# A graph layer on one Trainium2 core: a new order for the first blocks of edges

## Chip, core and metric

One core of a Trainium2 chip runs the whole kernel in one launch. The time is the device time of an execution in microseconds (us). The kernel before was run three times: 2399.72, 2402.55 and 2406.02 us, median 2402.55. The execution that was profiled took 2402.95 us, with a span of 2401.2 us from the first to the last instruction. Five engines work side by side, each in the order of its own instructions: TensorE (PE), VectorE (DVE), ScalarE (ACT), GpSimd (POOL) and SyncE (SP, which only issues transfers here).

## The reference

One layer of message passing over 12500 nodes with 64 features and 212500 edges, sorted by dst:

```python
h = jnp.maximum(_layernorm(x, axis=-1), 0.0)
edge_in = jnp.concatenate([h[src], h[dst], dist], axis=1)
e = silu(edge_in @ eW1 + eb1)
e = silu(e @ eW2 + eb2)
agg = segment_sum(e, src, num_segments=N)
out = silu(concatenate([h, agg], axis=1) @ nW1 + nb1) @ nW2 + nb2
return x + out
```

The first product is split: `eW1` has a part A for the source, a part B for the destination and a row for `dist`. A and B are multiplied with the nodes' h once, and each edge adds a row of A[src], a row of B[dst], dist times the last row, and eb1.

## The kernel before, in words

**Two halves.** Edges come sorted by destination but must be summed by source. So the kernel first *sends*: for each block of 1024 edges it gathers B's rows of their destinations, adds the share of dist and the bias, and scatters the 1024 rows into a table `q` in DRAM that is ordered by the bucket of the source (100 buckets of 125 nodes). Then *steps* load tiles of `q`, add A's rows, apply the two layers of SiLU and sum by node (`s_pt`, `s_p2`, `s_seg`, `s_add`). The buckets' places in `q` fill up level by level (14 levels), so steps of an early level run while later blocks are still being sent.

**A block.** 208 blocks of 1024 edges, two to a *pair*. `load(s)` fetches for a pair, by a base row number that SP reads from `base_i` (L355), the window `win` of B's rows: 2 x 60 rows at 4 offsets each, out of `tb0` for the first 30 blocks and out of `tb` later (L360). `load_rows(s)` puts two rows of edge weights (`ewH`, the weight rounded for the matmul, and `ewR`, what the rounding left) into `extras`, out of a DRAM copy `ews` (L335). `count(s)` finds each edge's row in q on VectorE: one-hot of the bucket (`oh`), its sum (`each`), a running count on TensorE (`upto`), the rank and the row number `to`; and it makes `pick`, the one-hot of the destination in the window plus the weight rows (L376). `send(s)` multiplies pick with win on TensorE (`qp`, L454), copies it to one of eight buffers `qs` on ScalarE (L466, L469), and issues one indirect write for each 128 edges on POOL (L476): 8 in a block, 1661 in all.

**The tables.** x is loaded in chunks of 12 nodes per partition (`xs`, three buffers), normed on VectorE and ScalarE (`norm`), turned on TensorE (`turned`, L682), and multiplied by A and B (`product`, L220 to L227); `ta`, `tb` and the h for the last layer `hd` are written to DRAM. Since the first blocks can't wait for all of it, the first 16 x 128 = 2048 nodes have a start of their own: `x0`, `first_rows(g)` for g = 0, 4, 8, 12, and a table `tb0` of B's rows alone (L696).

**The order** is written out by hand. PE, DVE, ACT and SP run their instructions in the order in which the program writes them (`manual_schedule`); only POOL's is chosen by the scheduler. Generators yield between stretches of work. The list `order` (L829 to L831) mixes the norm and the first rows, the sources' buckets (`sources(0)`, L768 to L781), the destinations (`destinations`, L744 to L763, which also makes `lo`, `base_i` and `rowsD`), the edge weights (`edge_weights`, L786 to L789: ewH on ScalarE, ewR - ewH and the two writes of ews on POOL) and then the first 1024 columns of the second half of the sources. Then come the small weights (POOL), the window of block 0, its count, and `send_all(0, 8)`: blocks 0 to 7, three pieces to a block, after each piece four steps of `feed`, which is the tables' work three chunks wide (`turns`), with `checks` after 48 steps. After these 24 pieces the bias of the second layer, `b2f`, is loaded and spread over 128 partitions by two matmuls of a row of ones and two copies (L854 to L859). A second stage of 39 pieces (blocks 8 to 20) follows with three feed steps to a piece, and then the main loop, in which pieces and steps alternate by a fixed plan of goals per level.

`checks` looks on VectorE whether every window held its destinations (two reductions over 104 x 2048, L796); if not, a general way at the end takes over, which these inputs don't need.

The eight `qs` are used in turn, so ScalarE's copy of a block's half waits until the indirect writes of eight halves ago have landed. Three buffers with the tag `rows` serve all of `got` and `rows_a`.

Of the kernel before, what the change touches and what calls it, by code (L numbers as in the profile page):

```python
# [34 lines left out]
OP = mybir.AluOpType  # L35
# [42 lines left out]
def tile_gnn(ctx: ExitStack, tc: tile.TileContext, x, src, dst, ew, eW1, eb1, eW2, eb2, nW1, nb1, nW2, nb2, out):  # L78
# [47 lines left out]
    CH = 12  # L126
    NE, EARLY = 16, 30
    x_rows = x.rearrange("(l b) d -> l b d", b=NB)
# [18 lines left out]
    nc.scalar.activation(warm, ones[:, 0:1], AF.Sqrt)  # L147
    nc.sync.dma_start(x0, x[: NE * P, :].rearrange("(p j) d -> p j d", j=NE))
    vec = lambda v, lo_, n, m: bass.AP(tensor=v.tensor, offset=v.offset + lo_, ap=[[m, n], [1, m]])
# [58 lines left out]

    tb0 = dram.tile([P * NE, 2 * H], F32, name="tb0")
    ta_buckets, tb_buckets = (t.rearrange("(l b) f -> l b f", b=NB) for t in (ta, tb))  # L210

# [39 lines left out]
    nb2b = const.tile([P, D], F32, name="nb2b")  # L251

    def later_weights():

        nc.gpsimd.dma_start(w2, eW2)
        nc.gpsimd.dma_start(w1g, nW1[D:, :])
        nc.gpsimd.dma_start(w2n, nW2)
        nc.gpsimd.dma_start(nb1c, bass.AP(tensor=nb1.tensor, offset=nb1.offset, ap=[[1, P], [1, 1]]))
        nc.gpsimd.dma_start(nb2b, rows_of(nb2, P))
        for a in range(2):  # L260
            nc.gpsimd.dma_start(w1n[a * D : (a + 1) * D, :], nW1[:D, :])
# [42 lines left out]
    with ExitStack() as work:  # L304
# [23 lines left out]
        def load_rows(s):  # L328

            if s < nblocks:  # L330
                p, g = s // 2, s % 2
                if g == 0:
                    for a in range(2):
                        at = a * HB + WL
                        nc.sync.dma_start(extras[p % 2][at : at + 2], ews[:, p, :, a])  # L335
# [11 lines left out]
        def load(s):  # L347

            if s < nblocks:
                p, g = s // 2, s % 2  # L350
                win = wins[p % NW]
                table, end = (tb0, NE * P) if s < EARLY else (tb, NB * P)
                assert s < EARLY or len(done_b) == NB // G
                if g == 0:
# [334 lines left out]
        def first_rows(g):  # L689

            hr = turned(x0, g)
            yield
            got = fp.tile([P, G, 2, H], F32, name="got", tag="rows")
            yield from product(1, hr, mm, "mm", got)
            yield
            nc.sync.dma_start(  # L696
                tb0.rearrange("(p j) f -> p j f", j=NE)[:, g : g + G, :], got.rearrange("p g k h -> p g (k h)")
            )
            yield
# [42 lines left out]
        def destinations():  # L742

            lim = lp.tile([NP, 1], F32, name="lim")  # L744
            nc.vector.tensor_scalar(lim, part[:NP], EARLY / 2 - 0.5, float((NB - NE) * P), op0=OP.is_gt, op1=OP.mult)
            nc.vector.tensor_scalar(lim, lim, float(NE * P - SPAN), None, op0=OP.add)
            nc.scalar.copy(f, dstR)
# [44 lines left out]
        def checks():  # L792

            ends = lp.tile([NP, 2, 4], F32, name="ends")
            for i, (op, sign, limit) in enumerate(((OP.max, 1.0, WL - 0.5), (OP.min, -1.0, 0.5))):
                nc.vector.tensor_reduce(ends[:, i, :], fv, AX.X, op)  # L796
                nc.vector.tensor_tensor(ends[:, i, :], ends[:, i, :], lo, op=OP.subtract)
# [20 lines left out]
        with listing:  # L818
            todo = groups()
            for _ in range(2):  # L820
                list(todo.pop(0))
            lists_, rows_, src0, src1, weights = destinations(), norm(x0, NE), sources(0), sources(1), edge_weights()
            made = [first_rows(g) for g in range(0, NE, G)]
            next(rows_)
# [26 lines left out]
        aggT = aggp.tile([P, NB, L], F32, name="aggT")  # L851
        b2f = aggp.tile([P, G, H], F32, name="b2f")
        eb2r = b2f[0:1, 0, :]
        for t in range(G):  # L854
            nc.sync.dma_start(b2f[0:1, t, :], rows_of(eb2, 1))
        for _ in range(2):
            p2 = p2p.tile([P, G, H], F32, name="p2")
            nc.tensor.matmul(p2, ones, b2f[0:1], start=True, stop=True)
            nc.scalar.copy(b2f, p2)  # L859
        ld2 = work.enter_context(tc.tile_pool(name="ld2", bufs=NQ))  # L860
# [197 lines left out]
```

## Time and profile before

| what | value |
|---|---|
| profiled execution / its span | 2402.95 us / 2401.2 us |
| median of three runs (lowest, highest) | 2402.55 us (2399.72, 2406.02) |
| busy: PE / DVE / ACT / POOL | 2084.7 / 1807.1 / 1316.8 / 1655.6 us |
| chain that ended last, by engine | PE 43%, DMA 19%, POOL 10%, DVE 7%, issue 5%, ACT 4% |
| DRAM traffic | 572.33 MB, mean 238 GB/s |
| first and last indirect write (L476) | start at 43.52 and 2209.16 us |

How to read it: a row of the timeline gives start, duration (both us), engine, line, operation, `out<-in`, and in brackets how long the engine had been idle and what ended that. A row of the waits gives the total us, the number of times and the longest. A row of the groups gives the line, engine, operation, names and count, then busy us, mean ns of one, and the idle time before it with its causes. A row of the windows gives the stretch and its length, then the engines' busy time in it with the number of instructions, the granted TensorE clock, the mean share of the DMA engines and GB/s. "SPq" is a transfer's issue on SP's queue. Buffer numbers are left out of names, so `tb` can be tb0, and `x` x0.

### The profile page before, as it was taken

How to read it: one execution, taken by the hardware profiler on the slowest of the kernel's cores; microseconds unless marked ns; L12 is line 12 of the kernel's file. 1: busy time of each engine (PE TensorE's matmuls, PEld its weight loads, DVE VectorE, ACT ScalarE, POOL GpSimd, SP SyncE). 2: the span in 40 equal slices, each digit the busy share in tenths (PEclk: the TensorE clock that was granted, in tenths of full speed). 3: DMA queues.
4: the chain of work that ended last, by engine and by line, in shares of the span. 5: the costliest groups of instructions: out<-in, count | busy, mean ns of one | idle time of the engine just before them, and what ended most of it. 6: DMA issues, size and time to landing. Idle time of an engine off the chain costs nothing.

```text
span 2401.2 us, 47870 instructions
## 1 busy us (share of the span) xinstructions
PE 2084.7 (87%) x17025; PEld 1909.0 (80%) x17025; DVE 1807.1 (75%) x2852; ACT 1316.8 (55%) x2861; POOL 1655.6 (69%) x1723
## 2 busy tenths in 40 slices
PE   3777887666688889988999999999999999999997
PEld 2555676655588788888888999998999999999885
DVE  7989977766678787776877667899988888875221
ACT  3333444333355566656666767666666666666543
POOL 5667777777777777777777766777777777776110
PEclk9555698877889999999999999999999999999999
DMA  5565877666677666777777777988888888888663
GB/s 161 210 235 212 274 227 236 209 209 220 210 250 253 209 225 221 225 236 255 258 259 247 264 251 254 294 262 255 269 269 275 266 267 279 263 270 269 207 187 92
DMA packets 238859, 572.33 MB, mean 238 GB/s; under 512 B 46346, under 2 KB 98534, under 8 KB 238097
## 3 DMA queue, kind: packets, MB, share of 16 engines
q1 hardware_dynamic: 154598, 390.24, 51.8%
q0 software_dynamic: 54080, 124.64, 14.2%
q10 hardware_dynamic: 29936, 54.31, 6.9%
q8 instruction: 138, 2.26, 0.4%
q14 instruction: 107, 0.88, 0.1%
HBM read 356.62 MB, written 212.35 MB: 237 GB/s over the span
## 4 chain that ended last, share of the span: by engine, by line
PE 43%; DMA 19%; POOL 10%; DVE 7%; issue 5%; ACT 4%; SPq 1%; ACTq 0%; POOLq 0%; DVEq 0%
DMA q<-qs,to 16%; PE seg L636 10%; POOL q L476 10%; PE p L622 10%; PE pt L583 9%; PE pt L576 5%; PE qp L454 4%; PE lr L562 3%; DMA out_dram<-os 2%; PE bc L344 1%; ACT qs L466 1%; DVE one L605 1%; SPq L124 1%; ACT e L592 1%; DVE rank L414 1%
## 5 line engine op out<-in xcount | busy, mean ns | idle before, releaser
L476 POOL DMA_INDIRECT q<-qs,to x1661 | 1615.7, 973 | 565.5 <-issue 398.4
L583 PE MATMUL pt<-oneT,a 125*128 125x128 f32 (+1 forms) x2800 | 433.9, 293 | 143.1 <-ACT oneT L567 142.1
L592 ACT ACTIVATE e<-pt 128x512 f32<-128x512 f32 x450 | 268.8, 597 | 477.4 <-PE pt L583 471.9
L622 PE MATMUL p<-w,e 128*128 128x128 f32 x3600 | 513.4, 287 | 0.0
L636 PE MATMUL seg<-one,e 128*128 128x125 f32 x3600 | 508.9, 285 | 0.2 <-DVE aggT L647 0.2
L583 PEld LDWEIGHTS pt<-oneT,a 125*128 125x128 f32 x2800 | 365.8, 198 | 159.5 <-ACT oneT L567 157.8
L622 PEld LDWEIGHTS p<-w,e 128*128 128x128 f32 x3600 | 457.6, 198 | 22.4 <-issue 22.4
L636 PEld LDWEIGHTS seg<-one,e 128*128 128x128 f32 x3600 | 445.3, 195 | 28.7 <-issue 27.3
L466 ACT COPY qs<-qp 128x512 f32<-128x512 f32 x418 | 244.5, 586 | 392.3 <-DMA q<-qs,to 276.1
L647 DVE TENSOR_TENSOR aggT<-aggT,seg 128x500 f32<-128x500 f32 x325 | 218.5, 672 | 210.1 <-PE seg L636 208.0
L454 PE MATMUL qp<-win,pick 128*128 128x256 f32 x1664 | 329.1, 325 | 28.3 <-DVE pick L376 10.8
L605 DVE TENSOR_TENSOR one<-misc,qt 128x500 f32<-128x500 f32 x450 | 302.7, 673 | 60.0 <-PE seg L636 33.1
L395 DVE TENSOR_REDUCE each<-oh 128x100 bf16<-128x800 bf16 x208 | 321.1, 1544 | 7.2
L454 PEld LDWEIGHTS qp<-win,pick 128*128 128x128 f32 x1664 | 254.1, 213 | 48.2 <-issue 15.1
L576 PE MATMUL pt<-ident,qt 128*128 128x128 f32 x1800 | 276.5, 277 | 8.3 <-ACT qs L466 7.9
L626 ACT ACTIVATE e<-p 128x512 f32<-128x512 f32 x450 | 268.7, 597 | 25.6 <-PE p L622 25.2
L567 ACT CAST oneT<-lr 125x512 fp32r<-125x512 f32 x450 | 264.7, 588 | 12.8 <-PE lr L562 12.4
L616 ACT COPY p<-b2f 128x512 f32<-128x512 f32 x450 | 267.2, 594 | 0.0
L576 PEld LDWEIGHTS pt<-ident,qt 128*128 128x128 f32 x1800 | 209.6, 143 | 23.7 <-issue 12.2
L414 DVE TENSOR_REDUCE rank<-terms 128x8 f32<-128x864 f32 x208 | 219.0, 1053 | 7.2
L376 DVE SCALAR_TENSOR_TENSOR pick<-bc,same,extra 128x512 fp32r<-128x512 f32 x208 | 154.6, 743 | 82.4 <-PE bc L344 54.3
L412 DVE TENSOR_TENSOR terms<-oh,misc 128x800 f32<-128x800 bf16 x208 | 203.6, 979 | 6.2 <-PE misc L400 5.9
(142 smaller groups left out, 1662.8 us busy)
## 6 DMA issues: line engine op xcount, KB each, us to landing
a<-ta SPq DMA_DIRECT2D x350, 512.0 KB
qt<-q SPq DMA_DIRECT2D x250, 288.0 KB
qt<-q SPq DMA_DIRECT2D x100, 576.0 KB
q<-zeros ACTq DMA_DIRECT2D x25, 1080.0 KB
q<-qs,to POOLq DMA_INDIRECT x1661
win<-tb SPq DMA_DIRECT2D x208, 120.0 KB
tb<-got SPq DMA_DIRECT2D x29, 512.0 KB
q<-zeros ACTq DMA_DIRECT2D x20, 720.0 KB
```

Of the source, the lines that this page charges most:

```text
L395: nc.vector.tensor_reduce(each, oh.rearrange("p t b -> p b t"), AX.X, OP.add)
L454: nc.tensor.matmul(qp[:, t % 2, :k], halves(pick[:, t * P : (t + 1) * P]), halves(win[:, :k, v]), start=v == 0, stop=v == 1,)
L466: nc.scalar.copy(qs[:, ts, :k, :H], qp[:, ts, :k, :])
L476: ins = nc.gpsimd.indirect_dma_start(out=q[:], out_offset=bass.IndirectOffsetOnAxis(ap=to[:k, j : j + 1], axis=0), in_=qs[:k, t % 2, a, :] ...
L576: nc.tensor.matmul(pt[:, t, :], qt[:, j, :H], ident, is_transpose=True, start=t == 0, stop=False, skip_group_check=True)
L583: nc.tensor.matmul(pt[:, cols, :], halves(a[:L, b, i * H : (i + 1) * H]), halves(oneT[:, cols, :]), start=False, stop=i == 1, skip_group_c ...
L592: nc.scalar.activation(e1, pt, AF.Silu)
L605: nc.vector.tensor_tensor(one.rearrange("p (b j) l -> p b j l", j=n), spots[:, None, None, :].to_broadcast(wide), loc[:, tiles[0][1] : til ...
L616: nc.scalar.copy(p2, b2f)
L622: nc.tensor.matmul(p2[:, t, :], e1[:, t, :], w2, start=False, stop=t == G - 1, skip_group_check=True)
L626: nc.scalar.activation(e2, p2, AF.Silu)
L636: nc.tensor.matmul(item[2][:, b, :], e2[:, t, :], one[:, t, :], start=j < G, stop=j >= G * (n - 1))
```

## The change

- `x0` is loaded in two parts, so that group 0 (4 of the 16 nodes of a partition) holds the first 512 nodes; `tb0`'s first 512 rows are written from it as before, and a table of its own, `tb00`, too. Pairs 0 and 1 (blocks 0 to 3) take their windows from tb00; the limit of the base rows follows with one more comparison.
- Only group 0 of the first rows is made ahead of block 0; the other three come first in the feed, two at a time.
- Block 0's weight rows come straight from ewH and ewR in SBUF instead of from ews.
- The order ahead of block 0 is another: ewH and the destinations' copy f stand behind group 0's rows, the count of block 0 begins before the destinations are finished, the second half of the sources comes later, and the first two chunks of x are loaded after the window of block 0.
- b2f is a constant tile, loaded on POOL's queue ahead of w2, and spread in the middle of block 0's count.
- The tests' reductions are cut in four each, with a yield after each; they come after 40 instead of 48 steps of the tables.
- After the first three pieces two feed steps are taken, then four as before.

```diff
-    NE, EARLY = 16, 30
+    NE, EARLY, FIRST_PAIRS = 16, 30, 2
...
-    nc.sync.dma_start(x0, x[: NE * P, :].rearrange("(p j) d -> p j d", j=NE))
+    for j0, j1 in ((0, G), (G, NE)):
+        nc.sync.dma_start(x0[:, j0:j1], x[j0 * P : j1 * P, :].rearrange("(p j) d -> p j d", j=j1 - j0))
...
+    tb00 = dram.tile([P * G, 2 * H], F32, name="tb00")
...
+    b2f = const.tile([P, G, H], F32, name="b2f")
...
     def later_weights():
+        nc.gpsimd.dma_start(b2f[0:1], bass.AP(tensor=eb2.tensor, offset=eb2.offset, ap=[[0, 1], [0, G], [1, H]]))
...
-                if g == 0:
+                if s == 0:
+                    for i, v in enumerate((ewH, ewR)):
+                        for a in range(2):
+                            at = a * HB + WL + i
+                            of = v[0:1].rearrange("p (g a e) -> p g a e", g=2, a=2)[:, :, a]
+                            nc.sync.dma_start(extras[0][at : at + 1], of)
+                elif g == 0:
...
+                if s < 2 * FIRST_PAIRS:
+                    table, end = tb00, G * P
...
-            nc.sync.dma_start(
-                tb0.rearrange("(p j) f -> p j f", j=NE)[:, g : g + G, :], got.rearrange("p g k h -> p g (k h)")
-            )
+            j0, j1 = (0, G) if g == 0 else (G, NE)
+            rows = tb0[j0 * P : j1 * P, :].rearrange("(p j) f -> p j f", j=j1 - j0)[:, g - j0 : g - j0 + G, :]
+            for to in ([tb00.rearrange("(p j) f -> p j f", j=G)] if g == 0 else []) + [rows]:
+                nc.sync.dma_start(to, got.rearrange("p g k h -> p g (k h)"))
...
-            lim = lp.tile([NP, 1], F32, name="lim")
-            nc.vector.tensor_scalar(lim, part[:NP], EARLY / 2 - 0.5, float((NB - NE) * P), op0=OP.is_gt, op1=OP.mult)
-            nc.vector.tensor_scalar(lim, lim, float(NE * P - SPAN), None, op0=OP.add)
+            lim = lp.tile([NP, 2], F32, name="lim")
+            nc.vector.tensor_scalar(
+                lim[:, 0:1], part[:NP], EARLY / 2 - 0.5, float((NB - NE) * P), op0=OP.is_gt, op1=OP.mult
+            )
+            nc.vector.tensor_scalar(
+                lim[:, 1:2], part[:NP], FIRST_PAIRS - 0.5, float((NE - G) * P), op0=OP.is_gt, op1=OP.mult
+            )
+            nc.vector.scalar_tensor_tensor(
+                lim[:, 0:1], lim[:, 0:1], float(G * P - SPAN), lim[:, 1:2], op0=OP.add, op1=OP.add
+            )
+            lim = lim[:, 0:1]
+            yield
...
-                nc.vector.tensor_reduce(ends[:, i, :], fv, AX.X, op)
+                for j in range(4):
+                    nc.vector.tensor_reduce(ends[:, i, j : j + 1], fv[:, j : j + 1, :], AX.X, op)
+                    yield
...
-            order = [rows_, weights, rows_, made[0], src0, made[0], src0, made[1], made[0], made[0], src0, made[1], lists_]
-            order += [made[2], made[1], made[1], src0, made[2], lists_, made[3], made[2], made[2], src0, made[3], lists_]
-            order += [made[3], made[3], src0, lists_, src1]
+            order = [rows_, rows_, made[0], src0, made[0], src0, weights, lists_, made[0], made[0], src0, src0, lists_]
+            order += [lists_, src0, src0]
             for part_ in order:
                 next(part_)
+            load(0)
+            load_rows(0)
+            for part_ in (count0, lists_, src1, count0):
+                next(part_)
...
             later_weights()
-            before_count = {1: src1}
-            load(0)
-            load_rows(0)
-            for _ in count(0):
+            for _ in range(2):
+                p2 = p2p.tile([P, G, H], F32, name="p2")
+                nc.tensor.matmul(p2, ones, b2f[0:1], start=True, stop=True)
+                nc.scalar.copy(b2f, p2)
+            for _ in count0:
                 pass
+            for _ in range(2):
+                list(todo.pop(0))
             load(1)
             rest = turns(todo, 3)
-            feed = itertools.chain(itertools.islice(rest, 48), checks(), rest)
-            for _ in send_all(0, 2 * FIRST):
-                for _ in range(4):
+            feed = itertools.chain(turns(made[1:], 2), itertools.islice(rest, 40), checks(), rest)
+            for i, _ in enumerate(send_all(0, 2 * FIRST)):
+                for _ in range(2 if i < PIECES else 4):
                     next(feed, None)
```

In the built program POOL's order differs in three places: b2f's load stands ahead of w2's, all twelve writes of the last window rows (`win<-three`) stand ahead of ewR - ewH instead of nine, and nothing stands between the writes of ews and the first indirect write.

More of the change, by code (lines that the diff above doesn't have):

```diff
@@ L251, in tile_gnn @@
     nb2b = const.tile([P, D], F32, name="nb2b")
+    b2f = const.tile([P, G, H], F32, name="b2f")
+    eb2r = b2f[0:1, 0, :]
     def later_weights():
+        nc.gpsimd.dma_start(b2f[0:1], bass.AP(tensor=eb2.tensor, offset=eb2.offset, ap=[[0, 1], [0, G], [1, H]]))
         nc.gpsimd.dma_start(w2, eW2)
@@ L819, in tile_gnn @@
             todo = groups()
-            for _ in range(2):
-                list(todo.pop(0))
             lists_, rows_, src0, src1, weights = destinations(), norm(x0, NE), sources(0), sources(1), edge_weights()
             made = [first_rows(g) for g in range(0, NE, G)]
+            before_count = {1: src1}
+            count0 = count(0)
+            next(lists_)
             next(rows_)
@@ L851, in tile_gnn @@
         aggT = aggp.tile([P, NB, L], F32, name="aggT")
[L852 to L859, printed above, removed]
         ld2 = work.enter_context(tc.tile_pool(name="ld2", bufs=NQ))
```

## The prediction

> **What bounds the kernel now.** I read the page first, then GpSimd's (POOL's) waits, then its timeline, because one row of the page stands out: 1661 indirect writes, L476, on one in-order engine.
>
> ```profile
> POOL 5667777777777777777777766777777777776110
> L476 POOL DMA_INDIRECT q<-qs,to x1661 | 1615.7, 973 | 565.5 <-issue 398.4
> POOL q L476 <- ACT qs L469: 71.6, 42, 14.6
> POOL q L476 <- ACT qs L469: 41.6, 9, 14.6
> POOL q L476 <- ACT qs L469: 24.6, 16, 5.3
> ACT qs L466 <- DMA q<-qs,to: 222.2, 74, 9.4
> ```
>
> The second row: 973 ns each. The timeline below shows 0.30 us of issue between neighbours, so POOL at its fastest makes one write in 1.27 us. The row of 7s in the slices is therefore POOL at its limit. The three wait rows (whole span; 40 to 250 us; 1250 to 1700 us) say where it starved: 41.6 us at the start, 24.6 us around 1500 us, and 71.6 - 41.6 - 24.6 = 5.4 us elsewhere. The last row (200 to 1000 us) is the other side of it: ScalarE, and TensorE behind it, stood 222.2 us because the eight qs buffers were not yet written out. So from about 200 to 1250 us POOL sets the pace; what it gains before 200 us is carried on one for one. Later TensorE takes over in turns, but its order is fixed and hangs on POOL's, so it too starts earlier by as much.
>
> The starving, on POOL's timeline (start, duration, in brackets the idle time before):
>
> ```profile
> 43.52 1.90 POOL L476 DMA_INDIRECT q<-qs,to  x1 [14.59 <-ACT qs L469]
> 45.73 1.00 POOL L476 DMA_INDIRECT q<-qs,to  x1 [0.30 <-issue]
> ...
> 54.73 1.21 POOL L476 DMA_INDIRECT q<-qs,to  x1 [5.46 <-ACT qs L469]
> 64.26 0.97 POOL L476 DMA_INDIRECT q<-qs,to  x1 [3.87 <-ACT qs L469]
> 87.15 0.96 POOL L476 DMA_INDIRECT q<-qs,to  x1 [2.22 <-ACT qs L469]
> 113.57 0.97 POOL L476 DMA_INDIRECT q<-qs,to  x1 [6.36 <-ACT qs L469]
> 152.45 0.97 POOL L476 DMA_INDIRECT q<-qs,to  x1 [7.77 <-ACT qs L469]
> ```
>
> The first write starts at 43.52 us; the five later holes, less 0.30 each, are 5.16 + 3.57 + 1.92 + 6.06 + 7.47 = 24.2 us. Blocks 0 to 7 (64 writes) lie ahead of 152.45.
>
> **The change, part by part.** *The first write.* Its path in the kernel before:
>
> ```profile
> 16.74 1.90 ACT L786 CAST ewH<-ewR 104x2048 fp32r<-104x2048 f32 x1 [1.59 <-DMA ewR<-in_edge_weight_dram]
> 16.85 0.66 PE L682 MATMUL ht<-ident,x 128*128 128x128 f32 x2 [10.24 <-DVE x L675]
> 18.55 0.37 ACT L686 COPY hr<-ht 128x256 f32<-128x256 f32 x1
> 18.97 1.23 PE L220 MATMUL ab<-w,hr 64*128 64x128 f32 x8 [1.46 <-ACT hr L686]
> 19.32 2.49 POOL L243 DMA_DIRECT2D win<-three  x5 [0.36 <-DMA nb1c<-in_L_gnn_nb_dram]
> 20.22 0.65 ACT L224 CAST got<-ab 128x256 fp32r<-128x256 f32 x2 [1.31 <-PE ab L220]
> 21.41 9.86 SPq L696 DMA_DIRECT2D tb<-got  x4
> 21.48 0.15 DVE L746 TENSOR_SCALAR lim<-lim 104x1 f32<-104x1 f32 x1
> 21.55 0.52 ACT L781 ACTIVATE bkt<-tr 128x416 bf16<-128x416 f32 x1 [0.32 <-PE tr L780]
> 21.83 4.54 POOL L787 TENSOR_TENSOR ewR<-ewR,ewH 104x2048 f32<-104x2048 f32 x1
> 23.23 1.91 ACT L747 CAST f<-dstR 104x2048 f32<-104x2048 int32 x1
> 27.80 1.22 DVE L757 TENSOR_TENSOR rowsD<-f,lo 104x1024 bf16<-104x1024 f32 x1
> 30.28 0.23 ACT L755 CAST base_i<-lot 1x104 int32<-1x104 f32 x1
> 30.83 1.22 DVE L757 TENSOR_TENSOR rowsD<-f,lo 104x1024 bf16<-104x1024 f32 x1
> 36.95 0.17 DVE L416 TENSOR_SCALAR to<-rank 128x8 int32<-128x8 f32 x1
> 37.08 1.01 SPq L360 DMA_DIRECT2D win<-tb  x2
> 38.20 1.14 SPq L335 DMA_DIRECT2D extra<-ews  x4
> 40.42 0.75 DVE L376 SCALAR_TENSOR_TENSOR pick<-bc,same,extra 128x512 fp32r<-128x512 f32 x1 [3.30 <-DMA extra<-ews]
> L360 SPq FUSED_REGOPS  x24: 43/46/56, 33.0 to 254.6; - x24
> ```
>
> pick waits for extra, extra stands on SP behind win, and win waits for all four writes of tb0 (the last issued at 31.27, the gate open at 37.08). After the change only one group's rows are written first, into tb00. The two new lim operations (0.15 each, and one that moved) stand ahead of the norm on VectorE: +0.45. Then ht ends at 17.51 + 0.45 = 18.0; hr no longer stands behind ewH and ends at 18.4; ab 19.7; got 20.4. ScalarE goes on with ewH to 22.3, f to 24.2, two bkt to 25.3, base_i to 25.5. SP reads base_i some 2.5 us after it is made (30.51 to 33.0), so win is issued at 28.0; tb00, issued at about 21.9, has landed by then if it takes no more than the 5.8 us of tb0's last write. win is then there at 28.0 + 1.0 + 3 = 32.
>
> *VectorE* after f: lo and its three sums 0.7 (four small operations of the size of lim's), one rowsD 1.2, and from 30.83 to 37.12 in the old order the other rowsD with the whole count of block 0, 6.3 us: 24.2 + 0.7 + 1.2 + 6.3 = 32.4.
>
> *extra* for block 0 comes straight from ewH and ewR in SBUF, without the write to ews. But POOL now issues one more weight load (b2f) and three more win rows ahead of ewR - ewH, 0.50 each: 21.83 + 2.0 = 23.8, later than ewH's 22.3. It ends at 28.4; the four small loads, 1.14 to issue and 2.2 from the first issue to pick before, are in at 31 to 32. Here is the wait that the change adds: SP stands at the third of them until 28.4, with the xs loads and the windows of pairs 1 and 2 behind; none is used before about 45 us.
>
> So pick starts at about 32.4 instead of 40.42: **-8.0**. Bounds: -10 (VectorE's chain without the 1.9 of ewH ahead of f) and -4 (extra landing as slowly as tb0's last write, 5.8 us, beside the 1.7 MB of ews). I take the value worked out, since its pieces are rows.
>
> The Trainium skill, page "SBUF — State Buffer", section "Who interferes with whom", speaks against this order: a VectorE instruction with two inputs in SBUF and a GpSimd instruction that reads SBUF lock each other out for a whole instruction. ewR - ewH would now run beside rowsD, which has two such inputs. By that rule rowsD would wait until 28.4, the first write would come 3.5 us later, and the sum below would be 2384.5, within the forecast's own spread. No row of this trace has the two side by side: the two rowsD, both 1.22, ran after POOL's subtraction had ended.
>
> *The bias of the second layer* cost 7.47 us at 152.45: a load, two matmuls and two copies in ScalarE's and TensorE's order.
>
> ```profile
> 145.47 2.04 PE L858 MATMUL p<-b2f,ones 1*128 1x512 f32 x2 [4.83 <-DMA b2f<-in_L_gnn_eb_dram]
> ...
> 150.29 0.58 ACT L859 COPY b2f<-p 128x512 f32<-128x512 f32 x1 [2.16 <-PE p L858]
> ```
>
> Moved ahead of the first qp, the group takes 150.87 - 145.47 = 5.4 us at most. TensorE reaches it when VectorE is halfway through that 6.3 us, at about 29, so it ends by 34.4 at worst, and qp waits for pick until 33.2 anyway. Its load, third on POOL's queue, is issued ahead of the win rows at 19.32 and so long in; without this cover each us that it is late is one on the first write. **-7.5**, bounds -7.5 and -6.
>
> *The feed.* In the first stage VectorE is the bound: the windows are 43 to 152 us and 152 to 285 us (PE, PEld, DVE, ACT, POOL busy).
>
> ```profile
> 43.00:152.00 109.00, 73.66 (x328) 52.47 (x328) 91.00 (x156) 39.13 (x108) 64.90 (x64) 0.55 0.56 196
> 152.00:285.00 133.00, 104.24 (x528) 79.05 (x528) 125.94 (x219) 57.39 (x155) 101.43 (x103) 0.56 0.68 238
> L227 DVE TENSOR_TENSOR rows_a<-ab,rows_a 128x256 f32<-128x256 f32 x24 | 9.0, 415 | 0.6 <-ACT rows_a L224 0.3 <-issue 0.3
> L227 DVE TENSOR_TENSOR got<-ab,got 128x256 f32<-128x256 f32 x22 | 8.4, 417 | 3.2 <-ACT got L224 3.2
> L666 DVE TENSOR_TENSOR cen<-xs,mean 128x768 f32<-128x768 f32 x5 | 4.8, 958 | 0.2
> L796 DVE TENSOR_REDUCE ends<-f 104x4 f32<-104x2048 f32 x2 | 4.6, 2282 | 0.0
> ```
>
> 91.0 of 109, with the bias and the first wait in the rest. Before, 96 feed steps fall into it, 93 of them tables: 9.0 + 8.4, and norms of five chunks, four operations like cen's 4.8 and small ones, about 39 in all, 0.42 a step. After it there are 90 steps: 12 of the three remaining first rows (six subtractions of 0.42, 2.5 us), 11 of the tests (4.6 as before, in eight pieces), 67 of tables. 26 x 0.42 - 2.5 = **-8.4**. It holds as far as VectorE stays the bound: the 65th write came 108.9 us after the first; less 7.5 and 8.4 that is 93.0, so it comes at 35.5 + 93.0 = 128.5, while POOL alone would need 64 x 1.27 = 81.5 us, to 117. So 0 is the one bound (holes that come from ScalarE's order and not from VectorE's load), -20 the other.
>
> In the second stage the same steps come back: 10.9 us less the 9 steps (3.8) that slip into the main loop, so 7. There VectorE was busy 125.9 of 133 us while POOL ran without a hole (101.4 busy, 103 writes at 1.27 each after the bias), and part of the 125.9 was counting ahead, which filled the qs buffers. Part of the 7 finds room in that: between 0 and **+7**, and I take **+2**, since no hole is seen at this load.
>
> The split of x0's load, four small loads instead of two, and a second write of one group's rows (0.35 us on SP) lie beside waits of VectorE and SP: 0.
>
> **Sum**, against the profiled execution's own 2402.95 us (span 2401.2 and 1.75 around it; the median of the runs is 2402.55): -8.0 - 7.5 - 8.4 + 2 = -21.9, so **2381**.
>
> **The rivals.**
> *Half of it:* the holes of the first stage come from queues, not from load, and appear again with the first rows in place of the norms. Then only the start and the bias count, less a few us: 2402.95 - 15.5 + 4 = 2392. For it: each hole's row names ScalarE's qs as what came last. Against: VectorE's 91 of 109.
> *The change doesn't do what it says:* extra or tb00 lands as late as before, and the first write stays at 43.5. Only the bias moves: 2395.5. Against: three of four table writes are off that path.
> *All holes close:* POOL runs from 35.5 without a stop, so 8.0 + 24.2 = 32 us earlier: 2371. Against: VectorE's load.
> *Slower:* SP. The window of pair 2 waits on SP for the last first rows, and behind it on SP stand the writes that free the three table buffers; ScalarE's in-order copies then stop, qs with them, at 60 to 80 us. The price is the hold itself, 5.8 us when four table writes and ews shared the queues (31.27 to 37.08); it decides from 22 us on, when it has eaten the sum, and five such holds, 28 us, would give 2409. For it: the windows now follow the tables more closely. Against: twelve steps are done by the fifth piece, pair 2 is first used in the thirteenth.
>
> **How the numbers follow.** Forecast 0.58 (own range 2375 to 2388), half of it 0.17, all holes close 0.08, change not doing what it says 0.06, slower 0.11. The range leaves out the slower case and half of the fullest one: 2373 to 2397. About 0.3%, 7 us, is what a measurement of this kernel can tell from no change. Faster by more: 0.58 + 0.17 + 0.08 = 0.83; within: most of the 0.06 and a little of the slower case, 0.07; slower: 0.10.
>
> **What would show it.** Right: the first L476 write at 34 to 38 us, no hole of 7 us near b2f, the 65th write near 128 us, POOL's waits for qs before 250 us at 20 us less, and the last write earlier by as much as the end. Wrong: holes over 3 us between the 64th and the 168th write; DMA named ahead of qs in the first 80 us; ewR - ewH ending after 30 us; or a first stage that gains and a span that doesn't, which would mean that POOL is not what carries the start to the end.

## The result and the profile after

The kernel after took 2387.94 us (median of 6 runs, 2384.66 to 2392.63) beside 2403.01 us (6 runs, 2399.72 to 2406.02) for the one before: ratio 0.9939, 95% interval 0.9925 to 0.9952. The profiled execution took 2388.01 us with a span of 2386.2, so 14.94 us less; the forecast was 21.9 less (2381). The result lies inside its range, at the upper edge of the narrower one that the forecast gave its main case (2375 to 2388).

The page of the kernel after: the row of POOL's slices and the group of the indirect writes (line L490 now; L476 before).

```profile
POOL 5777777777777777777777766777777777775110
L490 POOL DMA_INDIRECT q<-qs,to x1661 | 1615.7, 973 | 548.6 <-issue 397.8
```

The same 1661 writes of 973 ns; the idle time before them fell from 565.5 to 548.6 us, by 16.9. POOL's waits for qs (whole span; 30 to 250 us; 1250 to 1700 us):

```profile
POOL q L490 <- ACT qs L483: 48.4, 45, 10.5
POOL q L490 <- ACT qs L483: 16.4, 6, 10.5
POOL q L490 <- ACT qs L483: 23.4, 14, 5.3
```

By these rows the first stretch is 25.2 us better (41.6 before), the last one 1.2 (24.6 before). But two of the idle times below, 3.45 and 2.73, now have another name behind the arrow (hr and got) and are missing from the 16.4. Added up by themselves, the first wait and the holes were 40.3 us before (14.59 + 5.46 + 3.87 + 2.22 + 6.36 + 7.77) and are 22.0 now: 18.3 less. POOL's timeline, every idle time over 0.6 us up to 140 us:

```profile
39.46 1.92 POOL L490 DMA_INDIRECT q<-qs,to  x1 [10.54 <-ACT qs L483]
...
48.67 0.96 POOL L490 DMA_INDIRECT q<-qs,to  x1 [3.45 <-ACT hr L700]
...
65.56 0.97 POOL L490 DMA_INDIRECT q<-qs,to  x1 [1.80 <-ACT qs L483]
...
89.48 0.97 POOL L490 DMA_INDIRECT q<-qs,to  x1 [2.78 <-ACT qs L483]
...
110.88 0.97 POOL L490 DMA_INDIRECT q<-qs,to  x1 [0.68 <-ACT qs L483]
...
123.50 0.97 POOL L490 DMA_INDIRECT q<-qs,to  x1 [2.73 <-ACT got L226]
```

The holes, less 0.30 each, are 9.9 us instead of 24.2, and the one of 7.5 us at the bias is gone. But the first write is at 39.46, not at 35.5. Why, the timeline of all engines shows:

```profile
22.49 1.91 ACT L771 CAST f<-dstR 104x2048 f32<-104x2048 int32 x1
23.35 4.52 POOL L811 TENSOR_TENSOR ewR<-ewR,ewH 104x2048 f32<-104x2048 f32 x1
24.87 4.09 DVE L781 TENSOR_TENSOR rowsD<-f,lo 104x1024 bf16<-104x1024 f32 x1
26.44 1.02 SPq L374 DMA_DIRECT2D win<-tb  x2
27.57 1.33 SPq L343 DMA_DIRECT2D extra<-ewH  x2
29.01 2.82 SPq L343 DMA_DIRECT2D extra<-ewR  x2
31.30 1.22 DVE L781 TENSOR_TENSOR rowsD<-f,lo 104x1024 bf16<-104x1024 f32 x1
34.36 2.07 PE L869 MATMUL p<-b2f,ones 1*128 1x512 f32 x2 [0.68 <-ACT b2f L870]
35.00 0.17 DVE L430 TENSOR_SCALAR to<-rank 128x8 int32<-128x8 f32 x1
36.38 0.75 DVE L390 SCALAR_TENSOR_TENSOR pick<-bc,same,extra 128x512 fp32r<-128x512 f32 x1 [1.21 <-DMA extra<-ewR]
```

f was ready at 24.4, where the forecast had 24.2. The first rowsD took 4.09 us, the second, after POOL's subtraction had ended at 27.87, took 1.22. The 2.87 between them is on VectorE's path, which was free for pick at 35.17 instead of 32.4.

The weight rows came later still. SP issued the window, then the two rows of ewH, and reached ewR at 29.01, when the subtraction was already over, so SP did not stand for it. The four issues took 4.26 us (27.57 to 31.83; 1.14 in the kernel before), and pick got its rows 4.55 us after the last of them, 7.4 after ewR's first. Meanwhile ews was being written: from 32.0 to 36.4 the DMA engines were busy 0.84 of the time. So pick waited 1.21 more, and started at 36.38 instead of 32.4. The later of the two ends counts here: the rows alone would have held pick until then, and VectorE's 2.87 lay hidden behind them.

Where the gain went, by the start of the n-th indirect write (shifts are taken before rounding):

| write | before, us | after, us | shift | forecast |
|---|---|---|---|---|
| 1st | 43.52 | 39.46 | -4.06 | -8.0 |
| 65th (end of the first stage) | 152.45 | 133.69 | -18.76 | -23.9 |
| 169th (end of the second stage) | 286.90 | 268.39 | -18.52 | -21.9 |
| 979th | 1319.39 | 1301.10 | -18.30 | |
| 1201st | 1622.28 | 1605.10 | -17.18 | |
| last | 2209.16 | 2192.24 | -16.93 | |
| end of the span | 2401.2 | 2386.2 | -14.94 | -21.9 |

### The profile page after: what moved, and what is told of

Same layout as the page of the kernel before. It is cut to its first block, busy times and chain, and to the rows that moved or that the text cites. A ratio compares the mean times of both kernels' runs of the same rounds, so it can differ in the third digit from the quotient of the medians.

```text
span 2386.2 us, 47866 instructions
## 1 busy us (share of the span) xinstructions
PE 2074.8 (87%) x17025; PEld 1900.8 (80%) x17025; DVE 1810.0 (76%) x2859; ACT 1316.6 (55%) x2861; POOL 1655.9 (69%) x1724
## 4 chain that ended last, share of the span: by engine, by line
PE 45%; DMA 18%; POOL 10%; DVE 9%; issue 6%; ACT 5%; SPq 1%; ACTq 0%; DVEq 0%; POOLq 0%
DMA q<-qs,to 15%; PE p L636 10%; POOL q L490 10%; PE seg L650 10%; PE pt L597 9%; PE qp L468 5%; PE pt L590 5%; PE lr L576 3%; DMA out_dram<-os 2%; PE bc L356 2%; ACT qs L480 1%; DVE terms L426 1%; DVE rank L428 1%; DVE oh L401 1%; ACT oneT L581 1%
## 5 line engine op out<-in xcount | busy, mean ns | idle before, releaser
L490 POOL DMA_INDIRECT q<-qs,to x1661 | 1615.7, 973 | 548.6 <-issue 397.8
L468 PE MATMUL qp<-win,pick 128*128 128x256 f32 x1664 | 327.3, 323 | 24.6 <-DVE rows_a L229 6.0
L401 DVE TENSOR_TENSOR oh<-misc,bkt 128x800 bf16<-128x800 f32 (+1 forms) x209 | 203.5, 974 | 2.4 <-ACT bkt L805 2.4
```

Source lines behind the costliest of these rows:

```text
L468: nc.tensor.matmul(qp[:, t % 2, :k], halves(pick[:, t * P : (t + 1) * P]), halves(win[:, :k, v]), start=v == 0, stop=v == 1,)
L490: ins = nc.gpsimd.indirect_dma_start(out=q[:], out_offset=bass.IndirectOffsetOnAxis(ap=to[:k, j : j + 1], axis=0), in_=qs[:k, t % 2, a, :] ...
```

## The experiments

The theory behind them: POOL's writes carry the start to the end; the first write was late because VectorE and POOL shut each other out for a whole instruction (the lock) and because SP took the weight rows last; the bias and VectorE's load made the rest of the first stage. The rivals: transfers alone set the first write; the bias hid or cost elsewhere; the feed's cost is a fixed sum that is paid wherever it goes. Below, "span" is that of the one profiled execution, and a shift of a write is against the kernel named. The first write moves between executions: with the start of the kernel after it came at 39.46, 39.74 (e4) and 40.42 (e7), with the start of e8 at 35.77, 35.55 (e10) and 37.90 (e9). The time from the first write to the 65th is steadier: 94.1 to 94.2 us in the kernel after, e2, e5 and e10, and 93.9 in e8.

**The bias alone (e1).** The kernel before, with b2f loaded on POOL's queue and spread in the middle of block 0's count; nothing else.

```diff
+        nc.gpsimd.dma_start(b2f[0:1], bass.AP(tensor=eb2.tensor, offset=eb2.offset, ap=[[0, 1], [0, G], [1, H]]))
...
-            for _ in count(0):
+            count0 = count(0)
+            next(count0)
+            next(count0)
+            for _ in range(2):
+                p2 = p2p.tile([P, G, H], F32, name="p2")
+                nc.tensor.matmul(p2, ones, b2f[0:1], start=True, stop=True)
+                nc.scalar.copy(b2f, p2)
+            for _ in count0:
                 pass
```

> The kernel before with one part of the change: the bias of the second layer loaded on POOL's queue with the small weights and spread in the middle of block 0's count. Theory (the bias's hole is a cost of its own, and POOL carries the start to the end): first write stays at 43.5 us, the 65th comes at 145 instead of 152.45, the last write and the span 7.5 us earlier: 2395.5. Rival (the hole would be filled by VectorE's load anyway): the 65th write 3 us earlier or less, 2400 or more.

2400.09 us (11 runs) beside 2403.78: ratio 0.9978 (0.9969 to 0.9987); span 2394.0, 7.2 less than before, in the fastest of the 11 runs. POOL's timeline at the 65th write:

```profile
142.83 0.97 POOL L479 DMA_INDIRECT q<-qs,to  x1 [0.31 <-issue]
144.11 0.96 POOL L479 DMA_INDIRECT q<-qs,to  x1 [0.30 <-ACT got L224]
```

The hole of 7.47 is gone; the other four are as in the kernel before (5.15, 3.57, 1.91, 6.03). The 65th write comes 8.34 us earlier, the first 0.82: the bias is worth 7.5 at that place. Of the total the medians show 3.7 us and the ratio 5.3 (3.1 to 7.5), so the expected 7.5 lies at the edge of the interval.

**The bias late (e3).** The kernel after, with the load and the spreading back behind the first 24 pieces.

```diff
-            for _ in range(2):
-                p2 = p2p.tile([P, G, H], F32, name="p2")
-                nc.tensor.matmul(p2, ones, b2f[0:1], start=True, stop=True)
-                nc.scalar.copy(b2f, p2)
             for _ in count0:
                 pass
...
+        for t in range(G):
+            nc.sync.dma_start(b2f[0:1, t, :], rows_of(eb2, 1))
```

> The changed kernel with the bias loaded on SP and spread after the first 24 pieces again, as before. Theory: a hole of 7 us comes back ahead of the 65th write, which is 5 to 7.5 us later than 133.69 (a part may be covered by halves that are ready in qs); span the same later, 2394. The first write stays at 39.5, since the bias was hidden there; a rival (the two matmuls stood in the way of the first qp) gives a first write 1 us earlier.

2392.97 us, ratio 0.9948 (0.9934 to 0.9961), span 2389.6. POOL's timeline:

```profile
140.65 0.97 POOL L489 DMA_INDIRECT q<-qs,to  x1 [8.30 <-ACT qs L482]
```

The hole is back, 8.0 us, and the 65th write 6.96 later than in the kernel after. The first write, 39.63, is no earlier: the bias had cost nothing ahead of it. So the forecast's cover holds in the kernel after: qp waited for pick. In e8 below, where pick ends at 33.19, qp starts at 33.49, behind the second of these matmuls (31.49 to 33.56): there 0.3 us of the bias shows.

**The subtraction on VectorE (e2).** The kernel after, with ewR - ewH ahead of `lo` on VectorE.

```diff
-            nc.gpsimd.tensor_tensor(ewR, ewR, ewH, op=OP.subtract)
+            yield
+            nc.vector.tensor_tensor(ewR, ewR, ewH, op=OP.subtract)
```

> The changed kernel with ewR - ewH on VectorE, ahead of lo, instead of on POOL. Theory (rowsD took 4.09 us because it was locked out while POOL subtracted): the first rowsD takes 1.22 again, the count of block 0 ends 2.2 us earlier (33.0 instead of 35.2), the first write 2 to 3 us earlier than 39.46, and the span by as much: 2385.5. Rival (block 0's weight rows land late because of the traffic of ews, whatever VectorE does): rowsD may shrink, pick still starts at 36 or later, first write 39 or later, 2388.

2386.47 us, ratio 0.9921 (0.9907 to 0.9934), span 2383.9. The timeline:

```profile
22.43 2.29 DVE L812 TENSOR_TENSOR ewR<-ewR,ewH 104x2048 f32<-104x2048 f32 x1 [0.97 <-ACT ewH L810]
25.08 1.22 DVE L781 TENSOR_TENSOR rowsD<-f,lo 104x1024 bf16<-104x1024 f32 x1
34.18 0.75 DVE L390 SCALAR_TENSOR_TENSOR pick<-bc,same,extra 128x512 fp32r<-128x512 f32 x1 [1.66 <-DMA extra<-ewR]
```

VectorE does it in 2.29 us while it would wait for f, rowsD is at 1.22 again, and the first write is at 37.27, the 65th at 131.34: 2.2 and 2.35 earlier than in the kernel after. VectorE was free for pick at 32.52, 2.65 earlier, but in both kernels it is the rows of ewR that end pick's wait. So the 2.2 is how much sooner these rows came: the writes of ews were issued at 22.69 and 25.02 instead of 27.81 and 28.36, the DMA engines were busy only 0.30 from 31.8 to 34.1, and pick got its rows 1.25 us after their last issue instead of 4.55. No run takes the lock away and leaves the rows where they were, so what the lock alone is worth at the first write is not shown. In the total the intervals of this kernel and the kernel after overlap.

**The subtraction behind the first rowsD (e5).** On POOL as in the kernel after, but held until the first rowsD is done. If the two engines exclude each other, the second rowsD must suffer instead.

```diff
+            sub = nc.gpsimd.tensor_tensor(ewR, ewR, ewH, op=OP.subtract).ins
+            tc.add_manual_dep(sub, first_gap[0], AFTER)
```

> The changed kernel with POOL's ewR - ewH held until the first rowsD is done. Theory (VectorE and POOL lock each other out, instruction by instruction, where VectorE reads two inputs from SBUF): the first rowsD takes 1.22 us instead of 4.09; POOL subtracts from 26.1 to 30.6; oh (one input in PSUM) and each stay at 0.98 and 1.5 beside it; the second rowsD, which then starts beside it at about 28.7, takes 2.5 to 3.5. Rival (rowsD was slow for another reason, such as waiting for lo): the first stays at about 4, the second at 1.22. The first write: within 1.5 us of 39.5 in either case.

One run, 2387.32 us; span 2385.5. The timeline:

```profile
24.64 1.22 DVE L783 TENSOR_TENSOR rowsD<-f,lo 104x1024 bf16<-104x1024 f32 x1
25.78 0.98 DVE L401 TENSOR_TENSOR oh<-misc,bkt 128x800 bf16<-128x800 f32 x1
25.95 4.52 POOL L815 TENSOR_TENSOR ewR<-ewR,ewH 104x2048 f32<-104x2048 f32 x1 [1.85 <-DVE rowsD L783]
26.80 1.55 DVE L409 TENSOR_REDUCE each<-oh 128x100 bf16<-128x800 bf16 x1
28.25 3.30 DVE L783 TENSOR_TENSOR rowsD<-f,lo 104x1024 bf16<-104x1024 f32 x1
```

So it is. The subtraction ends at 30.47 and the second rowsD at 31.55, 1.08 us later, about as if it had begun only then; in the kernel after it was 1.09 (27.87 and 28.96). `oh` (one of its inputs, misc, lies in PSUM) and `each` (one input) ran beside the same subtraction in 0.98 and 1.55 us, the times they have elsewhere. The first write is at 39.06; here too pick waited last for the rows of ewR, 1.77 us.

**The weight rows ahead of the window (e8).** As the subtraction on VectorE, and SP takes block 0's weight rows before its window.

```diff
-            load(0)
             load_rows(0)
+            load(0)
```

> The kernel with ewR - ewH on VectorE (first write at 37.27), and on SP block 0's weight rows ahead of its window. Theory (of what was missing at the first write, 2.2 us were the lock and the rest the weight rows, which stood behind the window and landed beside the write of ews): pick no longer waits for extra and starts at 32.6 to 33.2 instead of 34.18; the first write at 35.6 to 36.6; the span about 1 us less than 2386.5. Rival: the window becomes the last (SP stands at ewR's load until 25, then at base_i), first write at 37 or later.

2383.73 us, ratio 0.9921 (0.9905 to 0.9938), span 2381.0. The timeline:

```profile
24.93 2.43 SPq L343 DMA_DIRECT2D extra<-ewR  x2
...
29.77 1.32 SPq L374 DMA_DIRECT2D win<-tb  x2
...
32.44 0.75 DVE L390 SCALAR_TENSOR_TENSOR pick<-bc,same,extra 128x512 fp32r<-128x512 f32 x1
...
35.77 1.66 POOL L490 DMA_INDIRECT q<-qs,to  x1 [10.44 <-ACT qs L483]
```

pick no longer waits for a transfer and starts at 32.44, the first write at 35.77, the 65th at 129.62. With the two overlooked waits taken away, the forecast's 32.4 and 35.5 come out, and the 65th write comes 1.1 us after its 128.5. In the total the interval still overlaps with that of the kernel after. Run again on another chip as e10, beside e9 below:

> The kernel of e8_rows_first once more, unchanged, on the same chip as e9: first write at 35.8 us, 65th at 129.6, median 2382 to 2385. It shows how far the end after the last write, 191 to 195 us so far, varies between executions of one program: if the 2 us between the kernels before and after are of that kind, it differs from e8's 191.6 by 1 us or more.

2382.45 us, ratio 0.9919 (0.9905 to 0.9933), first write 35.55, 65th 129.71. Here pick, again at 32.44, waited 0.35 us for the rows of ewR, so they come only just in time. From the end of the last write to the end there were 193.4 us, and 191.6 in the first execution: one program varies there by 1.8 us.

**Without tb00 (e6).** The kernel after, with all four groups of first rows ahead of block 0 and the first windows out of tb0.

```diff
-    NE, EARLY, FIRST_PAIRS = 16, 30, 2
+    NE, EARLY, FIRST_PAIRS = 16, 30, 0
...
-            feed = itertools.chain(turns(made[1:], 2), itertools.islice(rest, 40), checks(), rest)
+            feed = itertools.chain(itertools.islice(rest, 40), checks(), rest)
```

> The changed kernel without the table tb00: all four groups of first rows are made ahead of block 0, whose window waits for all four writes of tb0; the feed's 12 steps of first rows are taken by the tables. Theory (the window waited for the last of four writes): the first write falls back to 42 to 44 us, and the 65th by 2.5 to 5 us against 133.69; span 2391 to 2393. Rival (the direct load of the weight rows made the first write earlier, and the window would have been in time): first write at 40 or earlier, span within 2 us of 2388.

2399.81 us, ratio 0.9979 (0.9968 to 0.9989), span 2397.7. The timeline:

```profile
21.76 11.85 SPq L712 DMA_DIRECT2D tb<-got  x4
39.35 1.01 SPq L374 DMA_DIRECT2D win<-tb  x2
44.19 0.75 DVE L390 SCALAR_TENSOR_TENSOR pick<-bc,same,extra 128x512 fp32r<-128x512 f32 x1 [4.72 <-DMA extra<-ewR]
```

The direction was right, the size not: the window waits for the last of four writes, 5.7 us after its issue at 33.6, and the first write comes at 47.29, which is 3.8 us later than even in the kernel before. On SP the weight rows stand behind that window, and pick waited 4.72 us for them. The small table, together with the three other groups that it lets wait, carries most of the change: without the two 7.8 of the first write and 10.4 of the 65th are lost. This run does not part them.

**The tests undivided (e4).** The kernel after with two whole reductions.

```diff
-                for j in range(4):
-                    nc.vector.tensor_reduce(ends[:, i, j : j + 1], fv[:, j : j + 1, :], AX.X, op)
-                    yield
+                nc.vector.tensor_reduce(ends[:, i, :], fv, AX.X, op)
```

> The changed kernel with the tests' two reductions whole, as before, at the same place in the feed (so 8 feed steps fewer for them). Theory (a long run of VectorE's work in front of a count makes a hole): a hole of 4 to 6 us near the 48th to 56th write and the 65th write 2 to 4 us later than 133.69; span 2390 to 2392. Rival (only VectorE's load counts, and the load is the same): 65th write within 1 us, 2388.

2389.43 us, ratio 0.9934 (0.9920 to 0.9948), span 2390.1. POOL's timeline around the tests:

```profile
108.58 0.96 POOL L490 DMA_INDIRECT q<-qs,to  x1 [3.27 <-ACT qs L483]
...
136.75 0.97 POOL L490 DMA_INDIRECT q<-qs,to  x1 [1.06 <-ACT qs L483]
```

The 65th write is 3.06 us later than in the kernel after, 2.8 counted from the first write. The large hole is smaller and earlier than expected, 3.0 us (3.27 less 0.30) at the 45th write. The 8 steps saved go to the tables, but VectorE's busy time from the first to the 65th write is nearly the same, 84.3 us beside 83.9, which speaks for the long run as the cause and not for the load. The intervals of the medians overlap, so of the total nothing is shown.

**Fewer feed steps in the first stage (e7 and e9).** Three after a piece instead of four; in the first kernel the second stage takes four instead of three, in the second one (on top of e8) it stays at three and the rest slips into the main loop.

```diff
-                for _ in range(2 if i < PIECES else 4):
+                for _ in range(2 if i < PIECES else 3):
...
-            for _ in range(3):
+            for _ in range(4):
```

> The changed kernel with three feed steps to a piece instead of four in the first stage, and four instead of three in the second. Theory (VectorE's load makes the holes of the first stage): 21 steps of 0.42, 8.8 us, leave it, and the holes at the 17th, 33rd and 57th write (1.5, 2.48, 2.43) close, all but 1 us; the 65th write at 127 to 129 instead of 133.69; the second stage, at 127 of 132 us of VectorE's time, gives back 0 to 4; span 2382 to 2387. Rival (each hole is one norm that stands ahead of a qs in ScalarE's order, whatever the load): holes of the same size at other places, 65th write later than 132, span 2388.

2391.06 us, ratio 0.9948 (0.9932 to 0.9965), span 2388.4. POOL's timeline in the second stage:

```profile
231.73 0.97 POOL L490 DMA_INDIRECT q<-qs,to  x1 [2.71 <-DVE u L449]
...
239.87 0.97 POOL L490 DMA_INDIRECT q<-qs,to  x1 [3.35 <-ACT qs L483]
```

The 65th write came 88.5 us after the first instead of 94.2: VectorE's load does set the first stage, at 0.27 us a step for the 21 steps less. The second stage gave 7.7 back (shift against before -23.57 at the 65th write, -15.86 at the 169th), more than expected: four steps to a piece seem too dense there (e9, with three, has no such holes).

> The kernel of e8_rows_first with three feed steps after a piece in the first stage instead of four, and three in the second as before; the 21 steps left over go into the main loop. Theory (VectorE's load sets the first stage, and the second stage of e7 gave the gain back because four steps to a piece are more than VectorE has room for there): the first write stays at 35.8 us, the 65th comes 4 to 5 us earlier than in e8 (125 us), no hole over 1 us between the 65th and the 169th write, and the span is 4 to 5 us shorter, 2376 to 2377. Rival (the second stage's holes in e7 came from the tables' order being late for their readers, not from load): holes of 2 us and more show again near the 140th write or at the start of the main loop, and the span is 2380 or more.

2382.43 us, ratio 0.9908 (0.9892 to 0.9923), span 2382.7. The 65th write came at 125.59, and no hole over 1 us from there up to the 169th: the theory so far. The first write missed it: 37.90, with VectorE's subtraction already 1.5 us later than in e8. So the first stage took 87.7 us from first to 65th write instead of 93.9, 0.29 us for each step less. Then the rival's wait came, at the start of the main loop. ScalarE's and POOL's timelines:

```profile
285.04 0.65 ACT L226 CAST got<-ab 128x256 fp32r<-128x256 f32 x2 [6.25 <-DMA tb<-got]
285.57 0.60 ACT L581 CAST oneT<-lr 125x512 fp32r<-125x512 f32 x1
286.05 0.62 ACT L480 COPY qs<-qp 128x512 f32<-128x512 f32 x1
```

```profile
287.08 0.97 POOL L490 DMA_INDIRECT q<-qs,to  x1 [7.46 <-ACT qs L483]
```

ScalarE, in order, stood for a write of tb out of a table buffer, with qs behind it: what the forecast's slower rival described for SP and the table buffers, in another place. In the profile all 4 us and more are gone; between the medians of e9 and e10, run side by side, no difference shows.

**Four steps now and then (e11 and e12).** As e9, with four steps after every second (e11) or third (e12) piece of the second stage.

```diff
-            for _ in range(3):
+            for _ in range(4 if done % 2 == 0 else 3):
```

> The kernel of e9_three_three with four feed steps after every second piece of the second stage (three after the others): 19 of the 21 steps taken out of the first stage come back in the second, evenly. Theory (the first stage ends 4 us earlier for 21 steps less; e7 lost in the second stage because 39 more steps at its start are too dense, e9 at the start of the main loop because the last table writes came too late): the 65th write at 125 to 126 us, no hole over 1.5 us from there to the 400th write, 400th write at 555 to 557 us where e8's came at 559.8, span 2376 to 2378. Rival (the table work before the main loop is a fixed sum, and what leaves the first stage is paid again wherever it goes): holes of 3 us and more in all between the 65th and the 200th write, 400th write at 559 us or later, span 2380 or more.

> The same with four feed steps after every third piece: 13 of the 21 steps come back in the second stage, 8 slip into the main loop. Theory: as e11, or 400th write up to 3 us later if the last table writes still come too late for the start of the main loop. Rival: the hole at the start of the main loop is between nothing and e9's 7.2 us, with smaller ones ahead of it, 3 us and more together.

Inconclusive. On the chip that they came to, the kernel before itself took 3348.41 us (12 runs, 3332 to 3361); e11 took 3323.30, ratio 0.9932 (0.9902 to 0.9961), e12 3314.61, ratio 0.9899 (0.9866 to 0.9932). The expectations' absolute times can't be read there, and holes of 2 to 8 us run through both traces. Whether this mix is better than e8 stays open.

## Why the prediction was right or wrong

*The first write, -8.0: mis-sized; -4.06.* This is the step that failed. The forecast had the four small loads of weight rows "in at 31 to 32", from 1.14 us of issue and 2.2 "from the first issue to pick before", and "one rowsD 1.2" beside the subtraction on POOL. The runs put 4.26 of issue and 4.55 from there to pick in place of the first, so that pick could not start before 36.38, and 4.09 in place of the second, which made VectorE free at 35.17. By these ends the rows alone cost the 4.0 us at pick; the lock alone would have cost 2.8. The wait that the forecast did name, SP standing for the subtraction, did not come. The rule of the Trainium skill, page "SBUF — State Buffer", section "Who interferes with whom", was set against this and kept out of the sum because no row had the two side by side. The trace agrees with it: rowsD ended 1.09 us after the subtraction. That the first write came at 39.46, where the rule gave 39.0, is in part luck, since the wait that ended last was the one for the rows. The two kernels with the subtraction elsewhere (e2 and e5) show the lock from two sides. The bounds (-10 and -4) held only just; the far one was drawn from a slow landing beside the traffic of ews, and that is what came.

*The bias, -7.5: right.* Alone it moved the 65th write by 7.5 more than the first; put back it cost 6.96 there; and ahead of pick it hid in the kernel after. The forecast's own worst case, an end at 34.4, lay past the 33.2 that it named as cover; 0.3 of that shows in e8.

*The feed in the first stage, -8.4: right, a little large.* From the first write to the 65th there were 108.93 us and now 94.23; less the 7.5 of the bias, that is -7.2. e7 confirms that load counts, at 0.27 us a step where the forecast took 0.42. How the 7.2 divides stays open. VectorE's busy time between the two writes fell by 7.0 us (90.95 to 83.93), which would be load alone. But 26 steps of 0.27, less the forecast's 2.5, are only 4.5, and e4 gives 2.8 for the divided tests, which the sum had at nothing. By that account the size came out by luck.

*The second stage, +2: +0.2.* The 17 table steps that came back (26, less the 9 that slip into the main loop) found room at three to a piece, as the forecast thought, in the counting ahead: from the 65th to the 169th write VectorE made `oh` for 16 blocks before and for 13 now. At four to a piece, in e7, they did not.

*The rest at 0, and the small table:* e6 shows that tb00, with the other groups left for later, decides the start. The additional write itself took 0.43 us on SP (22.13 to 22.56), which next issued at 25.42; a cost of its own was not tried.

*The sum, "carried on one for one": nearly.* 18.5 us arrived at the 169th write and 18.3 at the 979th; then 1.4 were lost up to the last write and 2.0 behind it, 3.6 in all since the 169th (the forecast lost none). The 2.0 is of the size by which one program varies there (1.8, e8 and e10). Of the 1.4, 1.1 stands around the 1161st write, on POOL's timeline of before and after:

```profile
1570.85 0.97 POOL L476 DMA_INDIRECT q<-qs,to  x1 [0.64 <-ACT qs L469]
```

```profile
1554.09 0.96 POOL L490 DMA_INDIRECT q<-qs,to  x1 [2.12 <-ACT e L606]
```

The longer idle time, 2.12, was in ten of the twelve profiles on these chips, e1's too, the shorter, 0.64, only in before's and e3's. What decides between them was not tried.

So 21.9 - 14.9 = 7.0 is 3.9 of the first write, 1.2 of the feed, 3.6 of the late part, less 1.8 of the second stage, within rounding.

*The rivals.* "Half of it" lies nearer in time (2392), but not by its mechanism: the holes of the first stage did shrink. "All holes close": 9.9 us are left. "The change doesn't do what it says": no. "Slower": its mechanism came, later than it said and without its price. In the kernel after ScalarE stood 10.40 us for a write of ta out of a table buffer (0.20 is the longest such wait before, up to 290 us):

```profile
264.78 0.65 ACT L226 CAST got<-ab 128x256 fp32r<-128x256 f32 x2 [10.40 <-DMA ta<-rows_a]
```

POOL wrote on without a hole over 0.31 us there, out of the qs that were already filled. e2, e8 and e10 show the same stop, 9.9 to 10.1 us; in e9 the cover ran out.

*The forecast's own signs.* No hole at b2f, no hole over 3 us between the 64th and the 168th write, and the last write 16.9 us earlier beside an end 14.9 earlier: these came. The first write at 34 to 38 us and the 65th near 128 did not. The 20 us less of POOL's waits for qs came by the name of the wait (25.2), not by the holes themselves (18.3).

## What to carry to other kernels

When an edit moves work in time, list what will run beside it: a subtraction on GpSimd that cost nothing in one place cost VectorE 2.9 us in another, and VectorE itself could do it in 2.3 us of waiting time. When the first use waits for several transfers on one in-order queue, put the one whose data is ready first ahead, and let a small table carry the first windows. Of two waits that end close together, look which ends last: shortening the other one gains nothing yet. Work taken out of a crowded stage must have a place to go: here the second stage took 17 more steps for nothing at three to a piece, but not four to a piece.

## What the runs showed of the hardware that was not expected

*The clock row without effect.* From 70 to 270 us the windows (PE, PEld, DVE, ACT, POOL busy, granted clock, DMA share, GB/s) and then the group of the qp matmuls in the same stretch, first of before and then of after:

```profile
70.00:270.00 200.00, 147.81 (x676) 106.81 (x676) 181.12 (x318) 77.55 (x215) 141.00 (x143) 0.52 0.65 230
```

```profile
L454 PE MATMUL qp<-win,pick 128*128 128x256 f32 x160 | 48.4, 453 | 17.2 <-DVE rows_a L227 8.6 <-ACT qs L466 4.5 <-DVE got L227 1.6
```

```profile
70.00:270.00 200.00, 144.38 (x673) 107.20 (x674) 177.67 (x324) 75.81 (x216) 148.97 (x151) 1.00 0.66 236
```

```profile
L468 PE MATMUL qp<-win,pick 128*128 128x256 f32 x152 | 46.3, 456 | 19.6 <-DVE rows_a L229 6.0 <-ACT qs L480 6.0 <-DVE got L229 4.5
```

At 0.52 and 1.00 the same matmul took 453 and 456 ns. e8 and e10 are one program: they list 0.51 and 0.75 there, with 448 ns in both and the 65th write at 129.62 and 129.71. In this stretch, where TensorE waits for others, the row can't be taken for a cause.

*A chip 1.39 times slower.* e11's page, the chain of work and the indirect writes:

```profile
PE 53%; another core or an unknown queue 15%; ACT 10%; issue 7%; DVE 4%; DMA 2%; SPq 1%; POOL 1%; ACTq 0%; DVEq 0%; POOLq 0%
...
L490 POOL DMA_INDIRECT q<-qs,to x1661 | 1614.1, 972 | 1480.2 <-ACT qs L483 983.0
```

One write still takes 972 ns, and `one` on VectorE 673 as ever; what grew are TensorE's matmuls (seg 305 ns a piece instead of 285 in e8) and above all idle time, 15% of the chain of a kind that the profile can't name. The mean granted clock was 0.83 there and 0.92 in e8; whether that is the cause was not tried. The ratio to the kernel before stayed near that of the other chips; the absolute time says nothing across them.
